# Attention heads: even and odd key tiles on the two row halves, and scores moved up to 896 columns at a time

## The chip, the cores and the metric

The kernel runs on one core of a Trainium2 chip. The metric is the device time of one execution in microseconds; the figure given for a kernel is the median of its runs. A core has five engines that each work through their own instructions in order: TensorE (PE, with its weight loads as PEld), VectorE (DVE), ScalarE (ACT), GpSimd (POOL) and SyncE (SP, which issues most DMAs). PE writes to PSUM, eight banks of 512 f32 columns on each of 128 rows; everything else here lies in SBUF or DRAM.

## The reference

The input is 3327 rows of 256 numbers and an adjacency matrix. Two layers run one after the other. Layer 0 is a graph convolution and a mixture of experts with the best two of eight; layer 1 is a graph attention and then the part that matters here, `_L1_ffn_ref`: causal attention with four heads of width 64, where each head has one key and one value projection but four query projections ("experts"):

```python
q = jnp.einsum('bnsd,neod->bneso', sx, wq)      # 4 heads, 4 experts each
k = jnp.einsum('bnsd,nod->bnso', sx, wk)
v = jnp.einsum('bnsd,nod->bnso', sx, wv)
scores = jnp.einsum('bnesd,bntd->bnest', q, k) * d ** 0.5 + causal
att = jax.nn.softmax(scores, axis=-1)
qkv = jnp.einsum('bnest,bntd->bnesd', att, v)
```

The four experts' results are mixed by a gate, added to the head's own input, normalised, sent through two small linear layers and normalised and gated again. All of it is in f32.

## The kernel before

The rows are padded to 26 tiles of 128 (`NT`, `P`). The graph layers and the expert layer come first and are the same in both kernels, except that the value rows are stored for the heads in another order (`keep_values`, line 914). The heads stage is `heads` (line 999 on).

A *unit* is one query tile `t` and one head `h`: 104 units, in order of `t`. A unit has the keys of tiles 0 to `t`. `span` cuts them into `t // 4 + 1` *chunks* of at most four tiles (512 columns). For each chunk:

- `fill` (PE): scores `pqk`, one matmul for each of four experts, 128 queries by up to 512 keys, contraction 64. Keys stand twice, on rows 0 to 63 and again on rows 64 to 127 (`kt`, `wk` has its columns twice). Queries of experts 0 and 2 stand on the upper half of the rows, of 1 and 3 on the lower. So two experts' matmuls run side by side on the two halves of PE. Each expert's scores take one PSUM bank of the four in the pool `ps`.
- `drain` (DVE): takes each expert's scores out of PSUM to the score buffer `sc` and keeps the row maximum (`mx`); in a unit's last chunk it adds the causal mask as well. After the last chunk a reduction gives `anmax`, the negative maximum over the unit.
- `weigh` (ACT): the exponentials, in place, one instruction per expert, with their sums in `den`.
- `values` (SP): four DMAs that bring the chunk's value rows `vr` from DRAM; three buffers.
- `turn` (DVE): transposes the whole chunk, four experts at once, in 32x32 blocks.
- `attend` (PE): products of weights and values in 32-row pieces, added up in `po` (four more banks).

After a unit's last chunk `over` takes `po` out and `back` turns it with `ptO`. Two generators run beside the units, a step at a time: `prepare` (with `heads_of`) makes the next tile's keys, values and queries (`psxt`, `pv`, `pk`, `pq`), and `tail` finishes a tile (gates, norms, `ph`, `pfg`). Their small matmuls use the same four banks; `empty` takes them out of PSUM, on ACT or DVE by a running estimate of both loads.

The order of the instructions on every engine is the order in which this program writes them (`InOrder`, line 50, holds each engine to it). The main loop goes over the chunks: in round `k` it drains up to `wanted(k)`, attends chunk `k`, turns chunk `k + 1`, loads the values of chunk `k + 2`, weighs chunk `k + 2`, and ends with the fill of the next chunk. `extra(k)` moves weighing and turning one round further ahead for units of tile 5 up to about tile 23. Chunks of the next unit are drained early, since the exponentials need the maximum over the whole unit; that is what the nine score buffers of 512 columns are for.

Of the kernel before, what the change touches and what calls it, by code (L numbers as in the profile page):

```python
# [12 lines left out]
F32 = mybir.dt.float32  # L13
# [5 lines left out]
ALU = mybir.AluOpType  # L19
# [11 lines left out]
NEG = -1e30  # L31

# [17 lines left out]
class InOrder:  # L50
# [44 lines left out]
    def __init__(self, tc):  # L95
        nc = tc.nc
        self.tensor, self.vector = self.Engine(tc, nc.tensor), self.Engine(tc, nc.vector)
        self.scalar, self.gpsimd = self.Engine(tc, nc.scalar), self.Engine(tc, nc.gpsimd)
        self.sync = self.Engine(tc, nc.sync)


class Net:
# [811 lines left out]
    def keep_values(self, nc, vs, t, v):  # L914

        for b in range(4):
            nc.sync.dma_start(
                out=vs[:, :, 4 * t + b, :].rearrange("h r d -> r h d"),
                in_=v[ds(32 * b, 32), :].rearrange("p (h d) -> p h d", h=4),
            )  # L920

    def heads_fixed(self, one, nc):
# [50 lines left out]
        for k in range(2):  # L973
# [12 lines left out]
        mask = one.tile([P, BLK], F32, name="mask")  # L986
# [4 lines left out]
            out=mask[:, BLK - P :], in_=mask[:, BLK - P :], compare_op=ALU.is_ge, fill=NEG, base=0,  # L991
# [7 lines left out]
    def heads(self, xs, vs, out):  # L999
# [3 lines left out]
        with ExitStack() as ctx:  # L1003
            one = ctx.enter_context(tc.tile_pool(name="at", bufs=1))
            self.work = ctx.enter_context(tc.tile_pool(name="atw", bufs=2))
            scp = ctx.enter_context(tc.tile_pool(name="ats", bufs=9))
# [4 lines left out]
            ps = ctx.enter_context(tc.tile_pool(name="psm", bufs=4, space=PSUM))  # L1011
# [5 lines left out]
            kt = one.tile([P, 4, NP], F32, name="kt")  # L1017
# [82 lines left out]
            def heads_of(t, res, sxt, nz=None, v=None):  # L1100
# [11 lines left out]
                for c in range(2):  # L1112
                    for s in range(2):
# [3 lines left out]
                        )  # L1117
                for s in range(2):
                    empty(kt[:, s::2, ts(t, P)], pp[s], D)
# [3 lines left out]
                if t < AHEAD:  # L1123

                    qt = scp.tile([P, 4, BLK], F32, tag="sc", name="qts")[:, :, : 2 * P]
                    qt = qt.rearrange("p h (i q) -> p h i q", i=2)
                else:
                    qt = tl.tile([P, 4, 2, P], F32, tag="qt", name="qt")
# [9 lines left out]
                for s in range(2):  # L1138
                    empty(qt[:, s::2, :, :], pp[s], BLK, 8.0)
                yield  # L1140
                sx = tl.tile([P, D], F32, tag="sx", name="sx", bufs=4)
# [29 lines left out]
            def span(t, g):  # L1171


                n = t // 4 + 1
                lo, hi = (t + 1) * g // n, (t + 1) * (g + 1) // n
                return lo, hi - lo

            def fill(u, g):

                t, h = u["t"], u["h"]  # L1180
                lo, n = span(t, g)
                n *= P
                pq = u["pq"] = []
                for i in range(2):
                    pq += [ps.tile([P, BLK], F32, tag="b", name="pqk") for _ in range(2)]
                    for k in range(2):
                        r = ds(64 * k, 64)
                        nc.tensor.matmul(
                            pq[2 * i + k][:, :n], u["qt"][r, h, i, :], kt[r, h, ds(lo * P, n)],
                            start=True, stop=True,  # L1190
                        )

            def drain(u, g):

                n = span(u["t"], g)[1] * P
                last = g == u["t"] // 4
                if g == 0:
                    u["sc"] = {}
                    u["mx"] = sm.tile([P, 4, 8], F32, tag="mx", name="mx", bufs=3)
                sc = u["sc"][g] = scp.tile([P, 4, BLK], F32, tag="sc", name="sc")  # L1200
                for e in range(4):
                    s, m = u["pq"][e][:, :n], u["mx"][:, e, g : g + 1]
                    if last:
                        nc.vector.tensor_tensor_reduce(
                            sc[:, e, :n], s, mask[:, BLK - n :], 1.0, NEG, ALU.add, ALU.max, m
                        )
                    else:
                        nc.vector.tensor_scalar(
                            sc[:, e, :n], s, 1.0, None, ALU.mult, ALU.max, accum_out=m
                        )  # L1210
                    load["dve"] += 0.12 + 0.00104 * n
                if last:
                    u["nmax"] = sm.tile([P, 4], F32, tag="nmax", name="anmax")
                    nc.vector.tensor_reduce(
                        u["nmax"], u["mx"][:, :, : g + 1], AX.X, ALU.max, negate=True
# [3 lines left out]
            def weigh(u, g, experts):  # L1219

                n = span(u["t"], g)[1] * P
                q = ready[u["t"]]
                if u["h"] == g == 0 and 0 in experts:
                    q["den"] = sm.tile([P, 16, 7], F32, tag="den", name="aden", bufs=3)
                for k in experts:
                    e = u["sc"][g][:, k, :n]
                    nc.scalar.activation(
                        e, e, AF.Exp, bias=u["nmax"][:, k : k + 1],
                        accum_out=q["den"][:, 4 * u["h"] + k, g : g + 1],
# [3 lines left out]
            def values(u, g):  # L1233

                lo, n = (4 * i for i in span(u["t"], g))
                v = u["v", g] = vrp.tile([P, 16, 64], F32, tag="vr", name="vr")
                for q in range(4):
                    nc.sync.dma_start(out=v[ds(Q * q, Q), :n, :], in_=vs[u["h"], :, lo : lo + n, :])

            def turn(u, g):  # L1240


                n = span(u["t"], g)[1] * P
                w = u["sc"][g][:, :, :n]
                nc.vector.transpose(w, w)
                load["dve"] += 0.1 + 0.00417 * n
# [7 lines left out]
            def attend(u, g):  # L1254


                t = u["t"]
                w, v = u["sc"][g], u["v", g]
                lo, n = (4 * i for i in span(t, g))
                for b2 in range(0, n, 2):  # L1260
                    for k in range(2):
                        for q in range(4):
                            r, b = ds(Q * q, Q), b2 + k

                            after = 4 * t + q - lo
                            if b > after and t:
                                continue
                            nc.tensor.matmul(
                                po[ds(64 * k, 64), q, :, :], v[r, b, :], w[r, :, ts(b, Q)],
                                start=(g == b2 == 0), stop=(b + 2 > after if t else b2 == 2),  # L1270
                            )
# [133 lines left out]
            def tail(t, sx, qkv, glp, den):  # L1405
# [3 lines left out]
                nc.vector.tensor_reduce(rd, den[:, :, : t // 4 + 1], AX.X, ALU.add)  # L1409
# [104 lines left out]
            def last_shares(u):  # L1514
# [3 lines left out]
                    rd, ready[u["t"]]["den"][:, ds(4 * u["h"], 4), : u["t"] // 4 + 1], AX.X, ALU.add  # L1518
# [39 lines left out]
            def last_half(c, r):  # L1558
# [12 lines left out]
                if c:  # L1571
                    pg = r["pg"] = ps.tile([P, 4], F32, tag="b", name="pfg")
# [37 lines left out]
            units = [dict(t=t, h=h) for t in range(NT) for h in range(4)]  # L1610
            chunks = [(u, g) for u in units for g in range(u["t"] // 4 + 1)]
# [19 lines left out]
            def fill_next():  # L1631
                nonlocal filled
                if filled < len(chunks):
                    u, g = chunks[filled]
                    if g == 0:
                        begin(u)
                    fill(u, g)
                    filled += 1

            def drain_to(n):  # L1640
                nonlocal drained
                while drained < min(n, len(chunks)):
                    if filled == drained:
                        fill_next()
                    drain(*chunks[drained])
                    drained += 1

            def extra(k):

                t = chunks[min(k + 3, len(chunks) - 1)][0]["t"]  # L1650
# [606 lines left out]
```

## Time and profile before

| what | value |
|---|---|
| median of 3 runs | 2826.27 us (2823.85 to 2828.45) |
| the profiled execution: time | 2829.15 us |
| the profiled execution: span | 2827.4 us |
| granted TensorE clock, mean | 0.982 |
| busy: PE / DVE / ACT / POOL | 2641.5 / 2374.8 / 1809.2 / 1119.6 us |
| drains without the mask | 1152, 653.2 us |
| drains with the mask | 416, 242.0 us |
| transposes of scores | 392, 816.2 us |
| exponentials | 1568, 1041.4 us |
| score matmuls `pqk` | 766.7 us |
| products `po` | 756.4 us |

Busy time is the sum of an engine's instruction records; matmuls are pipelined and their ends are modelled, so PE's is not exact. All recorded instructions carry line 61, the helper that issues them, so groups are told apart by their tiles. The first `anmax` starts 960.7 us after the span's start: from there on the heads run.

### The profile page before, as it was taken

What the parts mean: (1) busy time and instruction counts of PE and PEld (TensorE: products, weight loads), DVE (VectorE), ACT (ScalarE), POOL (GpSimd) and SP (SyncE); (2) the same over time, 40 slices, a digit from 0 to 9 for tenths busy, and PEclk for the clock granted to TensorE, in tenths of its full rate; (3) what the DMA queues carried; (4) which work ended last, traced back from release to release, by engine and by line L of the source; (5) the groups of instructions that cost most, each with busy time, mean ns of one, the idle gap of its engine ahead of it and who ended that gap; (6) DMA issues with size and microseconds to landing.
All of it is one profiled execution on the core that took longest, in us unless ns stands there. A gap on an engine that the chain in (4) does not pass through costs nothing.

```text
span 2827.4 us, 124885 instructions
## 1 busy us (share of the span) xinstructions
PE 2641.5 (93%) x53338; PEld 1959.8 (69%) x53338; DVE 2374.8 (84%) x5517; ACT 1809.2 (64%) x5161; POOL 1119.6 (40%) x1597
## 2 busy tenths in 40 slices
PE   7999988878989999999999999999999999999986
PEld 5888877767767776676666666666666666666654
DVE  5114643599999798999999999999999999999997
ACT  5541135555555577777777776777767777776774
POOL 5655744532243157654444333333223222222121
PEclk9999999989999999999999999999999999999997
DMA  7997568647775333433433443444434444434432
GB/s 268 378 383 241 192 224 261 208 177 265 272 264 185 94 91 94 118 106 113 117 110 113 121 123 109 121 117 122 117 115 119 121 119 117 124 118 119 117 105 80
DMA packets 257947, 449.28 MB, mean 159 GB/s; under 512 B 58768, under 2 KB 156432, under 8 KB 257264
## 3 DMA queue, kind: packets, MB, share of 16 engines
q1 hardware_dynamic: 245104, 417.11, 47.1%
q0 software_dynamic: 6480, 17.76, 1.6%
q8 instruction: 419, 6.86, 1.0%
q10 hardware_dynamic: 5808, 6.44, 0.7%
q14 instruction: 136, 1.11, 0.1%
HBM read 392.98 MB, written 25.88 MB: 148 GB/s over the span
## 4 chain that ended last, share of the span: by engine, by line
DVE 38%; PE 28%; ACT 3%; issue 1%; DMA 1%; POOL 1%; SPq 0%; POOLq 0%; DVEq 0%; ACTq 0%
DVE sc L61 34%; PE pqk L61 10%; PE po L61 9%; PE acc L61 3%; PE ptO L61 2%; ACT sc L61 2%; DMA pan<-in_adjt_dram 1%; PE psxt L61 1%; DVE p L61 1%; PE pq L61 1%; ACT sq L61 0%; PE pt L61 0%; PE ph L61 0%; DVE sg L61 0%; PE pk L61 0%
## 5 line engine op out<-in xcount | busy, mean ns | idle before, releaser
L61 ACT ACTIVATE sc<-sc,anmax 128x512 f32<-128x512 f32 (+3 forms) x1568 | 1041.4, 669 | 102.0 <-DVE anmax L61 102.0
L61 PEld LDWEIGHTS po<-sc,vr 32*64 32x64 f32 x43728 | 659.9, 131 | 298.7 <-issue 135.1
L61 DVE STREAM_TRANSPOSE sc<-sc 128x2048 f32<-128x2048 f32 (+3 forms) x392 | 816.2, 2082 | 9.2 <-ACT sc L61 9.1
L61 PE MATMUL po<-sc,vr 32*64 32x128 f32 x43728 | 756.4, 276 | 33.0 <-DVE sc L61 26.1
L61 PE MATMUL pqk<-kt,qt 64*128 64x512 f32 (+1 forms) x2944 | 766.7, 586 | 20.3 <-DVE fgs L61 7.2
L61 DVE TENSOR_SCALAR_CACHE_REDUCE sc<-pqk 128x512 f32<-128x512 f32 (+2 forms) x1152 | 653.2, 622 | 26.5 <-PE pqk L61 24.7
L61 PEld LDWEIGHTS pqk<-kt,qt 64*128 64x128 f32 x2944 | 315.0, 186 | 243.6 <-issue 84.2
L61 PE MATMUL acc<-wh,p 128*128 128x257 f32 x1352 | 308.5, 386 | 35.7 <-DVE p L61 35.5
L61 PEld LDWEIGHTS acc<-wh,p 128*128 128x128 f32 x1352 | 254.4, 191 | 89.8 <-DVE p L61 53.2
L61 ACT ACTIVATION_READ_ACCUMULATOR sc<-sc,anmax 128x1 f32 x1568 | 299.8, 191 | 0.0
L61 PE MATMUL acc<-y,pan 128*128 128x256 f32 x1352 | 296.0, 380 | 0.8 <-ACT rstd L61 0.5
L61 POOL TENSOR_TENSOR ot<-ot,sxd 128x512 f32<-128x512 f32 x83 | 106.1, 1278 | 440.0 <-ACT ot L61 434.9
L61 PEld LDWEIGHTS acc<-y,pan 128*128 128x128 f32 x1352 | 255.5, 190 | 35.2 <-ACT rstd L61 0.9
L61 DVE CUSTOM_DVE_ANT_0 sc<-pqk,mask 128x512 f32<-128x512 f32 (+3 forms) x416 | 242.0, 636 | 20.8 <-PE pqk L61 20.4
L61 ACT ACTIVATE u<-u,d 128x512 f32<-128x512 f32 (+1 forms) x182 | 125.1, 688 | 154.7 <-DVE u L61 154.7
L61 DVE SCALAR_TENSOR_TENSOR p<-pan,u 128x512 f32<-128x512 f32 (+1 forms) x182 | 127.6, 701 | 10.5 <-PE acc L61 6.0
L61 DVE SCALAR_TENSOR_TENSOR u<-bc,d 128x512 f32<-128x512 f32 (+1 forms) x182 | 136.2, 749 | 0.1
L61 ACT ACTIVATE ar<-ar 128x1664 f32<-128x1664 f32 x52 | 82.5, 1588 | 80.6 <-DMA ar<-in_adj_dram 80.6
L61 DVE TENSOR_SCALAR y<-y,dinv 128x256 f32<-128x256 f32 x26 | 14.0, 537 | 134.0 <-POOL dinv L61 133.8
L61 PE MATMUL ptO<-igw,ot 128*128 128x68 f32 x832 | 116.9, 284 | 4.4 <-DVE sc L61 2.1
L61 PEld LDWEIGHTS ptO<-igw,ot 128*128 128x128 f32 x832 | 102.6, 194 | 23.3 <-issue 15.4
L61 ACT COPY qkv<-ptO 128x272 f32<-128x272 f32 x103 | 39.3, 382 | 121.1 <-PE ptO L61 121.0
(381 smaller groups left out, 3196.9 us busy)
## 6 DMA issues: line engine op xcount, KB each, us to landing
vr<-vs SPq DMA_DIRECT2D x976, 128.0 KB
ar<-in_adj_dram SPq DMA_DIRECT2D x104, 832.0 KB
vr<-vs SPq DMA_DIRECT2D x544, 96.0 KB
pan<-in_adjt_dram SPq DMA_DIRECT2D x156, 256.0 KB
pan<-in_adjt_dram SPq DMA_DIRECT2D x26, 1024.0 KB
pan<-in_adjt_dram SPq DMA_DIRECT2D x20, 832.0 KB
w1e<-w SPq DMA_DIRECT2D x59, 256.0 KB
took<-places SPq DMA_DIRECT2D x59, 129.0 KB
```

The lines of the kernel that those rows point to most:

```text
L61: made = make(*args, **kw)
```

## The change

Keys and queries change their places on the rows, and the unit of work for DVE and ACT becomes wider.

- `kt` has half the columns: keys of even tiles stand on rows 0 to 63, of odd tiles on rows 64 to 127. The matmuls `pk` are as before; each copy into `kt` writes one half of the rows.
- Queries are needed on both halves. `qt` gets a further dimension, and two DMAs on SP in `heads_of` copy each half to the other. For tile 2 a part of `kt` that is still free serves as `qt`.
- `doubles(t)` cuts a unit's keys into `ceil((t + 1) / 7)` *doubles* of at most seven tiles (896 columns, `WIDE`). In a double the tiles of one parity are one half and those of the other parity the other. One expert's scores of a double are two matmuls, one per half, that run on the two halves of PE into two neighbouring banks, so that the columns lie side by side.
- The pool of four banks becomes two pairs (`Pairs`); small matmuls get half a pair each.
- Drains and exponentials take a whole double of one expert, up to 896 columns, in one instruction. The mask is 896 columns wide. Six score buffers of 896 columns take the place of nine of 512.
- Transposes, values and products go in *rounds*: one round for a double of at most four tiles, else one round for each half. Value rows are stored with even tiles first (`place`), and each half of a round is loaded with four DMAs.
- Scores are filled and drained in *pieces* of two experts, each with a round by which it is due; the main loop is written anew around that, and starts four rounds before the first product.

The core of the diff:

```diff
+WIDE = 7 * P
+def place(t):
+    return t % 2 * (NT // 2) + t // 2
+def doubles(t):
+    n = -(-(t + 1) // 7)
+    out = []
+    for d in range(n):
+        tiles = range((t + 1) * d // n, (t + 1) * (d + 1) // n)
+        halves = [[i for i in tiles if i % 2 == p] for p in ((t + 1) % 2, t % 2)]
+        out.append([h for h in halves if h])
+    return out
+class Pairs:
+    def pair(self, name):
+        self.rest = None
+        return self.pool.tile([P, 2, BLK], F32, tag="b", name=name)
+    def tile(self, shape, dtype, tag, name):
+        if self.rest is None:
+            both = self.pair(name)
+            v, self.rest = both[:, 0, :], both[:, 1, :]
+        else:
+            v, self.rest = self.rest, None
...
-            scp = ctx.enter_context(tc.tile_pool(name="ats", bufs=9))
+            scp = ctx.enter_context(tc.tile_pool(name="ats", bufs=6))
-            ps = ctx.enter_context(tc.tile_pool(name="psm", bufs=4, space=PSUM))
+            ps = Pairs(ctx.enter_context(tc.tile_pool(name="psm", bufs=2, space=PSUM)))
-            kt = one.tile([P, 4, NP], F32, name="kt")
+            kt = one.tile([P, 4, NP // 2], F32, name="kt")
...
+                r = ds(64 * (t % 2), 64)
                 for s in range(2):
-                    empty(kt[:, s::2, ts(t, P)], pp[s], D)
+                    empty(kt[r, s::2, ts(t // 2, P)], pp[s][r, :, :], D)
...
+                for k in range(2):
+                    nc.sync.dma_start(
+                        out=qt[ds(64 - 64 * k, 64), :, 1, :, :], in_=qt[ds(64 * k, 64), :, 0, :, :]
+                    )
...
-            def fill(u, g):
+            def fill(g):
+                u, d, experts = g["u"], g["d"], g["experts"]
+                halves = u["doubles"][d]
+                g["pq"] = []
+                for e in experts:
+                    pair = ps.pair("pqk")
+                    lo = BLK
+                    for i, tiles in enumerate(halves):
+                        k, n = tiles[0] % 2, P * len(tiles)
                         r = ds(64 * k, 64)
+                        if i < len(halves) - 1:
+                            to, lo = pair[:, 0, BLK - n :], BLK - n
+                        else:
+                            to = pair[:, 1, :n]
                         nc.tensor.matmul(
+                            to, u["qt"][r, u["h"], int(e % 2 != k), e // 2, :],
+                            kt[r, u["h"], ds(tiles[0] // 2 * P, n)], start=True, stop=True,
                         )
...
+            def turn(r):
+                w = r["u"]["sc"][r["d"]][:, :, ds(r["lo"], r["n"])]
                 nc.vector.transpose(w, w)
...
+                    for k in range(2):
+                        at = len(rounds) - 1 if single else len(rounds) - 2 + k
+                        pieces.append(dict(
+                            u=u, d=d, experts=(2 * k, 2 * k + 1), double=count, round=at,
+                            due=at - (2 if single else 3), first=first, lead=lead,
+                        ))
...
+            for g in pieces:
+                g["by"] = g["round"] - len(g["u"]["rounds"]) + 1 - g["lead"]
...
             def extra(k):
-                t = chunks[min(k + 3, len(chunks) - 1)][0]["t"]
-                return int(chunks[k][0]["t"] >= 5 and t // 4 + 1 <= 6 or chunks[k][0] is units[-1])
+                k = min(max(k, 0), len(rounds) - 1)
+                far = rounds[min(k + 8, len(rounds) - 1)]["u"]["t"]
+                return int(rounds[k]["u"]["t"] >= 5 and far <= 20 or rounds[k]["u"] is units[-1])
...
+            for k in range(-4, len(rounds)):
+                want = wanted(k)
+                drain_to(min(want, drained + 1))
+                if k >= 0:
+                    attend(r)
+                if drained < want and filled == drained:
+                    fill_next()
...
+                    turn(rounds[flipped])
                     flipped += 1
+                drain_to(want)
...
+                if filled == drained < wanted(k + 1):
                     fill_next()
```

## The prediction

> **What bounds the kernel now.** I read the page's busy shares and chain first, then busy time by stretch, then the timeline of the heads stage, then the chain inside one stretch. The first score maximum stands at 960.7 us, so the heads are the last 1865 us, and the change touches only them.
>
> ```profile
> PE 2641.5 (93%) x53338; PEld 1959.8 (69%) x53338; DVE 2374.8 (84%) x5517; ACT 1809.2 (64%) x5161; POOL 1119.6 (40%) x1597
> ...
> DVE 38%; PE 28%; ACT 3%; issue 1%; DMA 1%; POOL 1%; SPq 0%; POOLq 0%; DVEq 0%; ACTq 0%
> ```
>
> The 84% of DVE is a mean over stages. By stretch (us, then PE, PEld, DVE, ACT, POOL):
>
> ```profile
> 1400.00:1600.00 200.00, 194.03 (x5294) 135.15 (x5298) 191.93 (x463) 147.84 (x461) 89.15 (x120) 1.00 0.40 114
> 2000.00:2200.00 200.00, 194.39 (x5609) 131.01 (x5612) 194.46 (x416) 150.17 (x484) 61.86 (x85) 0.99 0.41 118
> 2200.00:2400.00 200.00, 197.70 (x5658) 133.51 (x5645) 199.00 (x426) 153.91 (x486) 57.70 (x79) 1.00 0.41 118
> ```
>
> Two engines are full at once; ACT has a quarter free. The prices come from the timeline (start, duration):
>
> ```profile
> 2600.56 0.69 DVE L61 TENSOR_SCALAR_CACHE_REDUCE sc<-pqk 128x512 f32<-128x512 f32 x1
> 2601.17 0.69 DVE L61 TENSOR_SCALAR_CACHE_REDUCE sc<-pqk 128x512 f32<-128x512 f32 x1
> 2601.79 0.69 DVE L61 TENSOR_SCALAR_CACHE_REDUCE sc<-pqk 128x512 f32<-128x512 f32 x1
> 2602.40 2.31 DVE L61 STREAM_TRANSPOSE sc<-sc 128x2048 f32<-128x2048 f32 x1
> 2605.55 0.56 DVE L61 TENSOR_SCALAR_CACHE_REDUCE sc<-pqk 128x384 f32<-128x384 f32 x1
> 2606.03 0.56 DVE L61 TENSOR_SCALAR_CACHE_REDUCE sc<-pqk 128x384 f32<-128x384 f32 x1
> 2606.51 1.77 DVE L61 STREAM_TRANSPOSE sc<-sc 128x1536 f32<-128x1536 f32 x1
> ```
>
> Drains start 0.61 us apart at 512 columns and 0.48 at 384: 0.133 us per key tile and some 0.08 fixed. PE's prices stand in the chain of 2000 to 2040 us:
>
> ```profile
> 2000.27 1.92 PE pqk L61 x8
> 2002.18 1.58 PE po L61 x93
> 2003.77 1.04 PE ptO L61 x8
> 2004.80 1.92 PE pqk L61 x8
> 2006.72 2.02 PE po L61 x125
> ```
>
> Eight score records (four experts in two passes each, two row halves side by side) over four tiles take 1.92 us, 0.24 per tile and pair of experts; the products of four tiles take 2.02, 0.51 per tile.
>
> **Drains.** The built program of the changed kernel holds 992 drains instead of 1568, over the same columns. 576 fewer at 0.075 us is -43 us of DVE. [...]
>
> **Transposes.** A double of 5 to 7 tiles is turned in two parts: 468 transposes for 392, each with about 0.07 us between its columns (2048 elements at 1.04 ns in a 2.23 us spacing leave 0.1; the 1536 form leaves less). +5 us. DVE's net is -38 us of some 1800.
>
> **Score matmuls.** Before, two experts ran on the two row halves over the same tiles, so both halves were always full. Now one expert's even and odd tiles share the halves, and the longer part sets the time. The built program has 208 experts' doubles of 4+3 tiles (4 steps instead of 3.5), 224 of 3+2 (3 instead of 2.5), 32 uneven ones at tiles 0 and 2; 448 of 3+3 lose nothing. That is 232 steps more on 2808; at 0.24 us, +56 us of PE. It lies beside DVE only as far as PE has room.
>
> **Which engine is then the floor.** Per head of query tile t I add the prices. PE: 0.49 per tile of scores, 0.51 of products, 1.04 for ptO, and 1.8 for a quarter of the tile's small matmuls (psxt 1.09, pv 0.64, pk 0.71, pq 1.16, two ph 0.71, four pt 0.39, pfg 0.51). DVE: drains, transposes, and 0.8 (1.3 below tile 16) for maxima and tails. The measured time of a head is the distance between maxima:
>
> ```profile
> 2408.12 0.18 DVE L61 TENSOR_REDUCE anmax<-mx 128x4 f32<-128x24 f32 x1
> 2435.68 0.18 DVE L61 TENSOR_REDUCE anmax<-mx 128x4 f32<-128x24 f32 x1
> 2466.21 0.18 DVE L61 TENSOR_REDUCE anmax<-mx 128x4 f32<-128x24 f32 x1
> ```
>
> Floors DVE/PE before, then after, then measured before (mean of a tile's four heads): t=9: 13.3/12.8, 13.1/13.8, 13.6. t=14: 19.0/17.8, 19.0/19.3, 18.6. t=19: 24.3/22.8, 23.8/23.8, 24.0. t=20: 25.8/23.8, 24.9/25.3, 26.4. t=23: 29.0/26.8, 28.6/26.8, 28.6. The larger floor, over all 104 heads, falls by only 15 us: at half the tiles PE becomes the larger. **-15 us.**
>
> **Waits when two floors meet.** Before, where the floors lie within 0.6 us (t=4 to 11) heads ran 0.55 us over the larger one on average; where DVE leads by over 1 us (t=12 to 24), 0.0. After, 10 of the 14 tiles from 12 on have floors within 0.9 us. 40 heads x 0.55 = **+22 us**; bounds 0 and +45 (double). The cause is visible in the rounds. With one drain piece of two experts and one transpose per round, DVE needs 2 x 2.03 + 2.23 + 1.7 = 8.0 us for a 7-tile double, PE 2 x 1.92 + 3.5 = 7.4 and 0.7 of small matmuls: no slack. For the same 7 tiles it was 8.3 against 7.0 + 0.7. PSUM remains four banks, now two pairs, and a small matmul takes half a pair that ACT must empty before the second expert's scores can be written; before, it took one bank in four, which the last expert waited for at about the same moment, so I charge nothing more for that.
>
> **Query copies.** Each query tile now also goes to the other row half by two DMAs on SP. For tiles 0, 1, 5, 6 and 8 the PE order has the first scores directly behind that tile's pq matmuls, and for tile 3 nearly so: PE waits for the landing.
>
> ```profile
> L61 SPq DMA_DIRECT2D sxd<-nz x104: 596/605/1773, 901.1 to 2557.3; - x104
> ```
>
> This copy from SBUF to SBUF is the nearest row: 0.6 us an issue, and in the packet records of 958 to 962 us the last landing follows the last issue by 1.15. Two issues and a landing are 2.4 us; six tiles, +14, less what DVE still has queued: **+10 us** (bounds 0, +14). From tile 9 on other work stands between; the cover is a round of 4 us or more. While SP holds a copy for ACT's qt, the next vr pieces stand behind it; they are read two rounds later, and without that cover each tile would pay another 1.2 us (two issues). [...]
>
> **Values.** SP issues vr pieces 0.46 us apart. A round with two halves in one buffer needs 8 issues: 3.7 us, and the tile's other 13 issues at 0.6 add 2 per head, 5.7 in all against heads of 5.2 to 6.6 at tiles 1 to 3. **+2 us** (0, +6). Elsewhere four issues fit a round.
>
> **Look-ahead.** The extra round of weighing and turning ahead now ends at about tile 20 instead of 23. Before, tile 24, the first without it, ran 0.75 us per head worse against its floor than tiles 21 to 23. Twelve heads, 9 us, partly counted in the waits: **+5** (0, +9).
>
> **Exponentials.** 992 instead of 1568 at some 0.3 us fixed (0.60 spacing at 384, 0.70 at 512) is -170 us on ACT, which is not the bound. What can return is PE's waiting for ACT to empty a bank:
>
> ```profile
> PEld pqk L61 <- ACT qt L61: 10.6, 28, 2.2
> PEld pqk L61 <- ACT qkv L61: 6.6, 11, 1.4
> PEld pqk L61 <- ACT sxt L61: 5.4, 16, 0.9
> ```
>
> With sx 4.5 that is 27 us in all, and each exponential gets longer (about 1.0 us), so **-4** (0, -13). The key copies (the same columns on half the rows), the wider mask and the reordered value rows cost nothing on the path: ACT, POOL and DMA (0.41 busy) cover them. Uncovered, the mask's 384 more columns would be 1.6 us once, by POOL's 1.09 us for a 128x256 row.
>
> Sum: -15 + 22 + 10 + 2 + 5 - 4 = **+20 us**. The profiled execution took 2829.15 us (span 2827.4 and 1.75 outside), 2.9 above the median 2826.27. 2849 on its scale is 2846 on the median's.
>
> **Rivals.**
> (a) Faster: DVE stays the bound and the fixed drain time comes off whole, 2826 - 38 = 2788. For it: DVE busy 199 of 200 in 2200 to 2400, and 3+3 doubles, nearly half of all, which cost PE nothing. Against it: PE is at 194 to 198 in the same stretches. It decides if small matmuls fit into PE's idle time without delaying the next scores, waits under 0.1 us per head. With half of the saving, 2807.
> (b) Gain and loss cancel: -15 and waits of +15, copies hidden: 2826.
> (c) Much slower: two PSUM pairs make DVE and PE take turns. If each of the 468 rounds shows 0.2 us more, 94 stands in place of the 22: 2918; from 0.05 us a round on it exceeds the forecast. For it: a pair comes free only after a whole drain of 1.0 us. Against: one transpose of 1.7 to 2.2 us per round lies between drains and covers the fill.
> (d) The change does not do what it says: excluded, the built program has 896-column drains and exponentials.
>
> **Chances.** Forecast 0.45, (a) with its half form 0.35, (b) 0.12, (c) 0.08. The measurement tells 0.2%, 5.7 us. The forecast's own range, from its bounds without all favourable ends at once, is 2828 to 2880. The range runs from (a) at 2787 to 2888; left out are a gain above DVE's own saving and most of (c). Faster 0.35, same 0.11 (most of (b)), slower 0.54.
>
> **What would show it.** Right: DVE's busy total down by about 38 and its share of the heads below 96%; PE idle under 2% from tile 12 on, PE's share of the chain up; heads at tiles 14, 9 and 15 longer than before, at 16 and 24 shorter; pqk waiting for a qt copy at the tiles named. Wrong: DVE still at 98% with shorter heads everywhere (a), or DVE waiting for pqk in every round (c).

## The result and the profile after

The changed kernel takes 3033.18 us, the median of six executions (3026.43 to 3039.57), against 2826.23 us before. The ratio is 1.073 (95% interval 1.071 to 1.075): 7.3% or 207 us slower. The forecast was 2846 us in a range of 2787 to 2888. The direction was right and the size was off by a factor of ten. Below, "so many us above before" is always a kernel's ratio less one, times 2826, so that runs from different chips can stand side by side. The profiled execution has a span of 3030.9 us and a mean granted clock of 0.957, against 0.982.

The page's busy totals of the changed kernel, and its chain by engine:

```profile
PE 2736.3 (90%) x54138; PEld 2036.5 (67%) x54138; DVE 2357.0 (78%) x4441; ACT 1659.2 (55%) x4009; POOL 1117.1 (37%) x1597
...
PE 35%; DVE 22%; ACT 5%; issue 2%; POOL 1%; DMA 1%; POOLq 0%; ACTq 0%; SPq 0%; DVEq 0%
```

DVE's total fell, by 18 us, and PE took the chain over from it (35% against 28%), as forecast. But the busy shares fell too: the new time is waiting, and work of PE at a lower clock. Busy time by stretch of the changed kernel shows where (us, then PE, PEld, DVE, ACT, POOL, PE's clock, DMA share, GB/s):

```profile
960.00:1100.00 140.00, 112.74 (x1372) 86.16 (x1372) 72.30 (x209) 49.88 (x170) 23.12 (x30) 0.66 0.26 67
1100.00:1400.00 300.00, 244.70 (x5010) 175.98 (x5016) 192.84 (x395) 154.42 (x438) 151.73 (x209) 0.87 0.30 83
1400.00:1600.00 200.00, 189.17 (x5006) 131.27 (x4990) 179.58 (x331) 130.88 (x347) 99.31 (x137) 1.00 0.42 116
2000.00:2200.00 200.00, 191.97 (x5541) 129.89 (x5522) 188.15 (x286) 132.23 (x348) 66.57 (x93) 1.00 0.43 120
2200.00:2400.00 200.00, 192.96 (x5531) 132.76 (x5522) 186.29 (x261) 127.84 (x320) 55.69 (x75) 1.00 0.43 123
```

From 2000 us on both engines stand at 93 to 96.5%, where they had 97 to 99.5% before. Early, DVE is busy for 52 to 64% of the time and the clock is at 0.66 and 0.87. The same 36 heads, from the first score maximum of tile 0 to that of tile 9, before:

```profile
960.73:1266.33 305.60, 290.12 (x6411) 211.84 (x6409) 268.51 (x747) 224.78 (x755) 180.26 (x249) 0.98 0.35 98
```

and after:

```profile
962.62:1405.33 442.71, 359.74 (x6509) 263.48 (x6508) 269.23 (x607) 208.23 (x618) 176.39 (x243) 0.81 0.29 78
```

So 137 of the 207 us are lost there, and 65 on tiles 9 to 25 (1561 us before, 1626 after). In the early part PE's busy time grew by 69.6 us and its idle time from 15.5 to 83.0. By an estimate from these two lines the growth of busy time is nearly all clock: 359.74 us at 0.81 hold 68 us of lost clock, 290.12 at 0.98 hold 6. What DVE waits for, in its costliest groups over the whole kernel (busy, mean ns | idle before, releaser):

```profile
L80 DVE STREAM_TRANSPOSE sc<-sc 128x1536 f32<-128x1536 f32 (+3 forms) x468 | 829.4, 1773 | 18.9 <-ACT sc L80 18.9
L80 DVE TENSOR_SCALAR_CACHE_REDUCE sc<-pqk 128x768 f32<-128x768 f32 (+3 forms) x576 | 506.1, 911 | 87.0 <-PE pqk L80 85.6
L80 DVE CUSTOM_DVE_ANT_0 sc<-pqk,mask 128x768 f32<-128x768 f32 (+6 forms) x416 | 356.6, 887 | 150.8 <-PE pqk L80 148.9
```

The drains before:

```profile
L61 DVE TENSOR_SCALAR_CACHE_REDUCE sc<-pqk 128x512 f32<-128x512 f32 (+2 forms) x1152 | 653.2, 622 | 26.5 <-PE pqk L61 24.7
L61 DVE CUSTOM_DVE_ANT_0 sc<-pqk,mask 128x512 f32<-128x512 f32 (+3 forms) x416 | 242.0, 636 | 20.8 <-PE pqk L61 20.4
```

The drains take 862.7 us, against 895.2, and wait 234.5 us for PE's scores, against 45.1. The list of DVE's waits in the heads (total, times, longest) has them, first before, then after, as

```profile
DVE sc L61 <- PE pqk L61: 45.0, 52, 5.0
DVE sc L80 <- PE pqk L80: 234.6, 225, 11.0
```

And PE waits for DVE: here is the timeline of one head of tile 8 (start, duration, in brackets the idle time before and its releaser):

```profile
1333.45 0.69 DVE L80 TENSOR_SCALAR_CACHE_REDUCE sc<-pqk 128x512 f32<-128x512 f32 x1
...
1333.92 1.14 PE L80 MATMUL pqk<-kt,qt 64*128 64x256 f32 x8
...
1334.70 2.31 DVE L80 STREAM_TRANSPOSE sc<-sc 128x2048 f32<-128x2048 f32 x1 [0.55 <-ACT sc L80]
1336.93 0.65 DVE L80 TENSOR_SCALAR_CACHE_REDUCE sc<-pqk 128x512 f32<-128x512 f32 x1
...
1337.75 1.10 PE L80 MATMUL ptO<-igw,ot 128*128 128x68 f32 x8 [2.70 <-DVE sc L80]
...
1339.41 0.66 PE L80 MATMUL ptO<-ident,xn 128*128 128x128 f32 x2 [0.57 <-ACT qkv L80]
1340.00 2.93 PE L80 MATMUL pqk<-kt,qt 64*128 64x256 f32 x8
1341.69 0.82 DVE L80 CUSTOM_DVE_ANT_0 sc<-pqk,mask 128x640 f32<-128x640 f32 x1 [3.48 <-PE pqk L80]
```

One chain of waits can be followed here. PE writes the second piece's scores at 1333.92, and both pairs are full. DVE turns first (2.31 us) and drains after it, so ptO, which needs a pair, waits 2.70 us. Then the second half of ptO's pair, a transpose of `xn`, waits 0.57 us until ACT has emptied the first half. Then the next scores of the same shape take 2.93 us where they took 1.14: the granted clock is 0.50 from 1338.7 to 1345.5 us, and half the clock alone would make 2.3 us of it. Meanwhile DVE waits 3.48 us.

### The profile page after: what moved, and what is told of

Same layout as the page of the kernel before. It is cut to its first block, busy times and chain, and to the rows that moved or that the text cites. A ratio compares the mean times of both kernels' runs of the same rounds, so it can differ in the third digit from the quotient of the medians.

```text
span 3030.9 us, 125050 instructions
## 1 busy us (share of the span) xinstructions
PE 2736.3 (90%) x54138; PEld 2036.5 (67%) x54138; DVE 2357.0 (78%) x4441; ACT 1659.2 (55%) x4009; POOL 1117.1 (37%) x1597
## 4 chain that ended last, share of the span: by engine, by line
PE 35%; DVE 22%; ACT 5%; issue 2%; POOL 1%; DMA 1%; POOLq 0%; ACTq 0%; SPq 0%; DVEq 0%
DVE sc L80 20%; PE pqk L80 14%; PE po L80 14%; PE ptO L80 3%; ACT sc L80 2%; PE pt L80 1%; PE pq L80 1%; PE psxt L80 1%; ACT qt L80 1%; PE pv L80 1%; ACT sq L80 1%; PE ph L80 1%; DMA qt<-qt 0%; ACT ot L80 0%; POOL qkv L80 0%
## 5 line engine op out<-in xcount | busy, mean ns | idle before, releaser
L80 ACT ACTIVATE sc<-sc,anmax 128x768 f32<-128x768 f32 (+6 forms) x992 | 880.9, 891 | 111.9 <-DVE anmax L80 111.7
L80 PEld LDWEIGHTS po<-sc,vr 32*64 32x64 f32 x43728 | 683.3, 133 | 316.9 <-issue 139.2
L80 PE MATMUL pqk<-kt,qt 64*128 64x384 f32 (+3 forms) x3872 | 824.4, 515 | 62.3 <-DMA qt<-qt 19.8
L80 DVE STREAM_TRANSPOSE sc<-sc 128x1536 f32<-128x1536 f32 (+3 forms) x468 | 829.4, 1773 | 18.9 <-ACT sc L80 18.9
L80 PE MATMUL po<-sc,vr 32*64 32x128 f32 x43728 | 802.6, 281 | 35.7 <-DVE sc L80 19.8
L80 DVE TENSOR_SCALAR_CACHE_REDUCE sc<-pqk 128x768 f32<-128x768 f32 (+3 forms) x576 | 506.1, 911 | 87.0 <-PE pqk L80 85.6
L80 PEld LDWEIGHTS pqk<-kt,qt 64*128 64x128 f32 x3872 | 369.1, 193 | 279.1 <-issue 53.4
L80 DVE CUSTOM_DVE_ANT_0 sc<-pqk,mask 128x768 f32<-128x768 f32 (+6 forms) x416 | 356.6, 887 | 150.8 <-PE pqk L80 148.9
L80 ACT ACTIVATION_READ_ACCUMULATOR sc<-sc,anmax 128x1 f32 x992 | 188.8, 190 | 0.0
L80 PEld LDWEIGHTS ptO<-igw,ot 128*128 128x128 f32 x824 | 106.6, 202 | 47.5 <-issue 21.1
L80 ACT COPY ot<-po 128x512 f32<-128x512 f32 x83 | 48.4, 583 | 159.9 <-PE po L80 153.0
```

The costliest lines, as they stand in the source:

```text
L80: made = make(*args, **kw)
```

## The experiments

A *claim* below is a tile that has been taken from the pool of PSUM banks and not yet given back. The theory after this reading, called "turns": two pairs in place of four banks make PE and DVE take turns, most in the rounds of up to four tiles, and the clock follows the pauses. Its rivals: the query copies, the order of the work, the clock by itself.

| kernel | median us | ratio to before (95%) | us above before |
|---|---|---|---|
| changed | 3033.2 | 1.073 (1.071 to 1.075) | 207 |
| changed, no query copies | 3010.0 | 1.064 (1.063 to 1.066) | 181 |
| changed, drains ahead of transposes | 3003.9 | 1.063 (1.061 to 1.065) | 178 |
| changed, both drains at the round's start | 2993.3 | 1.060 (1.056 to 1.063) | 169 |
| changed, small products in whole pairs | 3009.0 | 1.064 (1.062 to 1.067) | 181 |
| changed, tile 14's `ot` on DVE | 3025.2 | 1.071 (1.069 to 1.074) | 202 |
| changed, drains split at the half | 3074.7 | 1.088 (1.086 to 1.090) | 248 |
| before, banks as two pairs | 2910.4 | 1.029 (1.027 to 1.031) | 82 |
| before, pairs, small products in whole ones | 2888.7 | 1.022 (1.019 to 1.026) | 63 |

**Pairs alone, in the kernel before.** This is rival (c) by itself: `Pairs` put into the kernel before, and nothing else. A pair holds the scores of two experts here, in the changed kernel those of one.

```diff
-            ps = ctx.enter_context(tc.tile_pool(name="psm", bufs=4, space=PSUM))
+            ps = Pairs(ctx.enter_context(tc.tile_pool(name="psm", bufs=2, space=PSUM)))
...
                 pq = u["pq"] = []
+                ps.rest = None
```

> The kernel before, with nothing changed but how the four banks are handed out: as two pairs, small products taking halves, the scores of two experts one pair; drains stay at up to 512 columns, keys and queries as before. My forecast charged the pairs nothing: 2826 to 2835 us. Theory 'turns', with two pairs in place of four banks as the cause by itself: 2870 to 2950, a good part of it in tiles 1 to 8. If it stays below 2840, the cause lies in the new order of drains and fills or in the shapes, not in the pairs.

It took 2910 us, 82 above before. DVE's groups in this kernel:

```profile
L61 DVE TENSOR_SCALAR_CACHE_REDUCE sc<-pqk 128x512 f32<-128x512 f32 (+2 forms) x1152 | 654.9, 622 | 63.8 <-PE pqk L61 62.1
L61 DVE CUSTOM_DVE_ANT_0 sc<-pqk,mask 128x512 f32<-128x512 f32 (+3 forms) x416 | 242.5, 637 | 50.8 <-PE pqk L61 50.0
```

The drains' busy time is what it was before (653.2 and 242.0 us), and their waits for scores went from 45 to 112 us. The price lies on all tiles: 42 us by the first maximum of tile 9, 41 after it.

**Whole pairs for small products**, in the same kernel. A second product in a pair was written only after ACT had emptied the first; this takes that wait away and leaves the two claims.

```diff
             v, self.rest = both[:, 0, :], both[:, 1, :]
+            if name != "pqk":
+                self.rest = None
```

> The kernel before with its banks handed out as two pairs, as in the run that took 2910 us, but with every small product taking a whole pair for itself, so that none waits until ScalarE has emptied the other half. Theory 'halves' (the price of the pairs is the second product of a pair waiting for the emptying of the first): 2850 to 2890. Theory 'two where there were four' (the price is that only two claims on PSUM can be open at a time): a second product in the same round now needs the other pair, and the scores behind it wait longer; 2920 to 2990.

2889 us (2887 to 2908), 63 above before (53 to 74): the shared halves were some 20 us of the 82. That lies just inside what "halves" expected, but the greater part is left: 63 us with two claims where there were four, each given back only when both its banks are empty. In the pairs kernel PE's waits from tile 0 to 8 began with this line, which is not among the greater ones in the run with whole pairs:

```profile
PE ptO L61 <- ACT qkv L61: 13.4, 25, 1.6
```

The same edit in the changed kernel:

> The changed kernel with every small product in a whole pair of its own, as in the run of the kernel before with pairs that went from 2910 to 2889 us by it. Theory 'halves' (the second product of a pair waits for the emptying of the first): 3000 to 3020 us. Theory 'two claims' (with whole pairs the small products hold up the scores): 3040 to 3080.

3009 us, 25 less than the changed kernel, as "halves" expected, and the waits of ptO for ACT's `qkv` are no longer listed among PE's waits in tiles 0 to 8.

**The query copies**, left out:

```diff
-                for k in range(2):
-                    nc.sync.dma_start(
-                        out=qt[ds(64 - 64 * k, 64), :, 1, :, :], in_=qt[ds(64 * k, 64), :, 0, :, :]
-                    )
...
-                            to, u["qt"][r, u["h"], int(e % 2 != k), e // 2, :],
+                            to, u["qt"][r, u["h"], 0, e // 2, :],
```

> The changed kernel without the copies of the queries to the other half of the rows: every score product reads the first placement, so the scores of half the products use another expert's queries; the number and the shapes of all other instructions stay. My forecast priced the wait for the copies at 10 us, so 3033 - 10 = 3023 us. Theory 'turns' (most of the 207 us come from TensorE and VectorE waiting for each other over two pairs of banks, in the rounds of up to four tiles above all): 3005 to 3020, since 13.6 us of TensorE's idle time in tiles 1 to 8 end with the copies' transfers and the clock falls after some of them. Theory 'copies' (the waits for them set the early tiles' pace and the low clock there): 2960 or less, and a granted clock of 0.95 or more between 963 and 1405 us, against 0.81.

3010 us: 25 us less, and the clock of tiles 0 to 8 stays low (0.82). In the changed kernel these were PE's greatest waits in that stretch (total, times, longest):

```profile
PE pqk L80 <- DMA qt<-qt: 13.6, 5, 5.9
PE ptO L80 <- ACT qkv L80: 11.8, 23, 0.8
PE ptO L80 <- DVE sc L80: 10.7, 6, 2.8
PE pq L80 <- ACT qt L80: 6.3, 5, 1.4
```

The copies are the first line, and only one of many. In tile 6 the copies and the scores behind them are

```profile
1193.55 1.26 SPq L80 DMA_DIRECT2D qt<-qt  x2
1197.03 1.22 PE L80 MATMUL pqk<-kt,qt 64*128 64x384 f32 x2 [5.95 <-DMA qt<-qt]
```

From the first issue to the scores that wait it is 3.5 us (3.3 to 4.5 in tiles 0, 1, 5 and 8), where my sum had 2.4 for two issues and a landing.

**The order of drains and transposes.** First the transposes were moved behind the second drain:

```diff
+                drain_to(want)
                 while flipped <= min(k + 1 + extra(k), len(rounds) - 1):
...
                     flipped += 1
-                drain_to(want)
```

> The changed kernel with both pieces of a round drained before the round's transposes, in place of one before and one behind them. Theory 'turns': in the rounds of up to four tiles (tiles 0 to 3, 7, half of 8) ptO waits some 2.5 us a head for the transpose that stands ahead of the second drain; 12 + 16 + 4 rounds x 1 to 2.3 us fall away, 2980 to 3010 us, with heads 1 to 3, 7 and 8 shorter and the others as they were. If the waits come from something else, the order of these two makes no difference: 3025 to 3040.

3004 us, 29 less. Tiles 3, 7 and 8 got 1.8 to 2.7 us a head shorter; tiles 1 and 2, named as well, did not (9.4 and 8.9 us before the edit, 9.3 and 9.1 with it). Then both pieces were drained at the start of the round, which puts the second piece's scores ahead of the attention products:

```diff
-                drain_to(min(want, drained + 1))
+                drain_to(want)
```

> The changed kernel with both pieces of a round drained at once at its start, so that the second piece's products go ahead of the round's attention products on TensorE, in place of behind them. Theory 'turns': in the rounds of up to four tiles VectorE then goes from the first piece to the second without waiting for the attention products, and the transpose runs beside them: more than the 29 us that came of moving the transpose alone, 2970 to 2995 us, tile 7 under 15 us a head against 18.1. If the start and tile 7 are slow for another reason (the copies, the clock alone): 2995 to 3035.

2993 us, 38 less than the changed kernel. Tile 7 fell from 18.1 to 14.8 us a head and ptO's waits for DVE left the list. The order was part of the change, and my sum has no term for it.

The two first edits together, drains ahead of transposes and no copies:

> The changed kernel without the copies of the queries and with both drains ahead of the transposes: the two edits that gave 23 and 29 us by themselves. If they act in different places: 3033 - 52 = 2981 us, and 70 us remain above the kernel before with pairs (2910). If both cut the same pauses, in which the clock falls: 2990 to 3000. The scores of half the products use another expert's queries.

2980 us (1.053, 1.051 to 1.054), 58 less than the changed kernel, where the two by themselves give 25 + 29: they do not cut the same waits.

**The clock.** Products of zeros were put where PE waits, first ahead of ptO in tiles 4 to 8:

```diff
                 if ended:
+                    for q in range(8 if u["t"] < 9 and not r["ends"] else 0):
+                        nc.tensor.matmul(
+                            po_all[:, q % 4, :P], self.ident, mask[:, :P], start=False, stop=False
+                        )
                     back(ended)
```

> The changed kernel with eight products of zeros (128x128, adding nothing) ahead of ptO in the heads of tiles 4 to 8, where TensorE waits; some 20 x 8 x 0.28 = 45 us more work for TensorE. Theory 'the clock falls because TensorE stands still': the granted clock of tiles 4 to 8 goes from 0.83 to 0.92 up to 0.97 or more, the other rows get shorter by 30 us, and the time is 3010 to 3035. Theory 'the clock follows something else': it stays under 0.93 there and the time is 3050 to 3080.

3047 us (1.077, 1.076 to 1.079), between the two expectations. In tile 7 the clock rose from 0.86 to 0.98 and its four heads got 3.6 us shorter, with 9 us more to do; tiles 5 and 8 reached only 0.93 and 0.89, and tiles 4 and 6 did not change. Then eight such products (`start=True, stop=True`) ahead of each round's attention products in tiles 0 to 3:

> The changed kernel with eight products of zeros (128x128, overwritten after) ahead of the attention products of each round of tiles 0 to 3: 16 x 8, 36 us of work at full clock. Theory 'the clock falls because TensorE stands still too often': the granted clock of tiles 0 to 2 rises from 0.50 to 0.67 up to 0.9 or more and the time is 3020 to 3045, the added work paid by the rows that get shorter. If the clock of the first tiles follows something else: it stays below 0.7, and the time is 3065 to 3100.

3042 us (1.075, 1.073 to 1.077), in the range expected if the clock follows PE's pauses, though the clock stayed under the 0.9 expected there. Tiles 0 to 2 in the changed kernel:

```profile
957.62:1047.60 89.98, 75.65 (x804) 58.98 (x805) 45.51 (x149) 30.53 (x112) 11.39 (x15) 0.57 0.25 66
```

and with the added products:

```profile
961.29:1055.54 94.25, 78.45 (x964) 64.24 (x965) 45.03 (x149) 30.55 (x112) 11.40 (x15) 0.85 0.24 63
```

The 160 PE records more are 80 products of two records each, some 27 us of busy time, and the stretch got only 4.3 us longer, since the clock went from 0.57 to 0.85. Shown is, for tiles 0 to 2 (0.57 to 0.85) and tile 7 (0.86 to 0.98), that work in the pauses keeps the clock up, so that the lost clock there is a consequence of the pauses and no cause beside them. For tiles 4 and 6, where the added work left the clock as it was, this is argued and not shown.

In the trace of the changed kernel the clock goes between 0.50 and 1.00, with 0.81 as the mean of 443 us; the wait in the timeline above, before it went from 1.00 to 0.50, was 2.70 us.

**One late operand.** At tile 14 PE waits once for POOL, which has a norm's operations ahead of `ot`. The timeline of the changed kernel:

```profile
1777.68 0.56 ACT L80 COPY ot<-po 128x512 f32<-128x512 f32 x1
...
1782.34 0.72 POOL L80 TENSOR_TENSOR fo<-fo,fnb 128x256 f32<-128x256 f32 x1
1783.02 1.26 POOL L80 TENSOR_TENSOR ot<-ot,sxd 128x512 f32<-128x512 f32 x1
...
1784.34 1.98 PE L80 MATMUL ptO<-igw,ot 128*128 128x68 f32 x8 [4.48 <-POOL ot L80]
```

ptO then takes 1.98 us, not 1.10: the clock again, 0.50 at that time. The edit is `u["t"] < 5 or u["t"] == 14` in `over`, which gives this multiplication to DVE.

> The changed kernel with the multiplication of po by sxd in tile 14 on VectorE, as in tiles 0 to 4, in place of ScalarE and GpSimd: ptO no longer waits for GpSimd behind the tail's norms. In tile 14 it waited 4.5 us once, and the rows behind it ran at half the clock for some 10 us more: theory 'one late operand and the clock behind it cost 8 to 10 us': 3021 to 3027. If the wait is taken over by another one: 3030 to 3040.

3025 us, 5 less by the ratio and 8 by the medians. The intervals of the two ratios overlap; the heads show it more surely: tile 14 went from 23.8 to 21.9 us a head, 7.5 us for four.

**What the wider drains are worth.** Each drain was split in two at the boundary of the halves, with everything else kept:

```diff
                 for e, s in zip(g["experts"], g["pq"]):
+                    at = 0
+                    for i, tiles in enumerate(halves):
+                        w = P * len(tiles)
...
+                                to, s[:, ds(at, w)], 1.0, None, ALU.mult, ALU.max, accum_out=m
```

> The changed kernel with each double's scores emptied by one instruction per half and expert (up to 512 columns) in place of one per expert (up to 896): 976 more instructions on VectorE, some 73 us by the 0.075 us that I took for one's fixed part. By the floors of my forecast (VectorE's is the larger one from tile 12 to 25, 14 tiles x 4 heads x about 20 more instructions x 0.075 us) it loses 40 to 75 us: 3073 to 3108. Theory 'turns' (what an emptying saves is given back in waits for pairs): 10 to 35 us, 3043 to 3068.

3075 us, 41 more. DVE's groups here:

```profile
L80 DVE TENSOR_SCALAR_CACHE_REDUCE sc<-pqk 128x384 f32<-128x384 f32 (+2 forms) x1152 | 550.4, 532 | 69.2 <-PE pqk L80 67.7
L80 DVE CUSTOM_DVE_ANT_0 sc<-pqk,mask 128x384 f32<-128x384 f32 (+3 forms) x816 | 387.2, 527 | 145.0 <-PE pqk L80 143.5
```

The drains take 937.6 us, 74.9 more for 976 more of them: 0.077 us each, and 41 of the 75 us reach the end. That is the low end of what the floors expected, and "turns", which had 10 to 35 us, missed: the saving is not given back in waits to the extent that it held. The wider drains do what they should; the change loses in spite of them.

**Other cuts of the tiles.** Sevens and a rest (`tiles = range(7 * d, min(7 * d + 7, t + 1))`):

> The changed kernel with the tiles of a query tile cut into sevens and a rest in place of equal parts: tile 7 goes 7 + 1 in place of 4 + 4, tile 8 7 + 2 in place of 4 + 5, tile 14 7 + 7 + 1, tile 21 7 + 7 + 7 + 1; the number of doubles is the same. Theory 'turns': the rounds of four tiles with two drains and a transpose of 2.3 us between them are the worst ones (tiles 7 and 8 take 7 us a head more than before, tile 9 1.7), so tile 7 falls from 18.1 to about 15.5 us a head and tile 8 from 20.1 to about 17: 3005 to 3020. If the loss comes with each double and not with the rounds of four: 3028 to 3050, as the rest of one tile costs a transpose and a score step more.

3146 us (1.112, 1.110 to 1.113), far outside both expectations. Tile 8 fell from 20.1 to 17.8 us a head, but tile 7, which should have fallen, rose from 18.1 to 19.7, and tiles 10, 11, 18 and 21 to 24 rose by 2.2 to 5.2. It has fewer rounds (432 for 468), so the number of rounds alone is not what is paid for. Rounds of unlike width in a row may be; that was not tried by itself.

**All mends together.** Both drains at the start, whole pairs, and tile 14's `ot` on DVE in one kernel; then the same without the copies:

> The changed kernel with three edits at once: both pieces drained at a round's start (40 us by itself), small products in whole pairs (24 us), tile 14's multiplication on VectorE (8 us). If they act apart from each other: 3033 - 72 = 2961 us. If they cut the same pauses, in which the clock falls: 2975 to 2995. If the loss above the kernel before came from these alone it would reach 2889 or less, which I do not expect: two claims on PSUM in place of four took the kernel before from 2826 to 2889 with none of the change's other parts.

2966 us (1.047, 1.045 to 1.049), 133 above before; single edits, 38 + 25 + 5 less than 207, would give 139.

> The same three edits, and the copies of the queries left out (23 us by itself; the scores of half the products use another expert's queries). Apart from each other: 2938 us. What then remains above the kernel before with whole pairs (2889 us) is the price of the uneven rounds and of the doubled score products, less the 42 us that the wider emptying saves: 2938 leaves 49 us for it. Below 2915 the four edits and the two claims are all there is; above 2955 the edits overlap.

2946 us (1.040, 1.037 to 1.043), 112 above before; the sum would be 114. The four edits add up. The copies are part of what the kernel needs, so this last one only measures. Nearly all that the four give lies in tiles 0 to 8, which went from 443 to 361 us (before: 306). Tiles 9 to 25 went from 1626 to 1619 us, against 1561: the late loss is hardly touched by them. In the kernel before, pairs alone added 41 us to those tiles, and with whole pairs 31.

**Sixes.** The kernel with three mends, with `if t in (8, 9, 14, 15, 21): tiles = range(6 * d, min(6 * d + 6, t + 1))`:

> The three edits that gave 2966 us, and tiles 8, 9, 14, 15 and 21 cut into sixes and a rest (6+3, 6+4, 6+6+3, 6+6+4, 6+6+6+4) in place of parts of four, five and six: where a double of five puts three tiles on one half of the rows and two on the other, TensorE works three steps for two and a half, and its two rounds are of three and two tiles. Tiles 9, 14, 15 and 21 lose 1.5 to 3.5 us a head against the kernel before. Theory 'doubles of five' (the step lost and the uneven rounds are what is left there): these four tiles get 1 to 2.5 us a head shorter, tile 8 stays or gains, 2925 to 2950 us. Theory 'any change of the width between rounds costs' (as the cut into sevens showed: 113 us more): no gain or a loss, 2960 to 3000.

2978 us (1.054, 1.051 to 1.057). In us per head:

| tile | before | changed | three mends | with sixes |
|---|---|---|---|---|
| 7 | 10.9 | 18.1 | 15.0 | 14.0 |
| 8 | 13.4 | 20.1 | 17.6 | 15.6 |
| 9 | 13.6 | 15.3 | 15.2 | 14.1 |
| 10 | 14.2 | 15.5 | 15.3 | 18.2 |
| 14 | 18.6 | 23.8 | 21.7 | 21.1 |
| 15 | 19.5 | 22.1 | 22.3 | 20.9 |
| 16 | 22.6 | 22.0 | 21.9 | 22.7 |
| 21 | 26.3 | 29.1 | 29.4 | 29.7 |
| 22 | 27.4 | 28.9 | 28.5 | 29.9 |

The column of three mends comes from its longest execution (2987.5 us), that of sixes from its shortest (2974.0), with a mean clock of 0.81 and 0.87 over tiles 0 to 8, so tiles 7 and 8 can't be compared closely. Tiles 9, 14 and 15 got shorter, by 12 us in all, and tiles 10, 16 and 22, where the number of rounds per head now steps up, got 20 us longer; tiles 9 to 25 together took 12 us more, as the medians do. The expectation of 2925 to 2950 fell; that of "any change of the width between rounds costs" holds. In the changed kernel, too, three of the worst tiles are those at which that number has just risen: 8 (from 2 to 3), 14 (from 4 to 6), 21 (from 6 to 8). At tile 7, the worst against before, it has not; there the number of doubles rises from 1 to 2. Drains are due a whole head ahead, so at such a step more scores must be written and drained in the rounds of the tile before; that this is the reason was argued from the code and not tried.

**The account.** 207 = 63 (two claims) + 25 (shared halves) + 38 (order) + 25 (copies) + 5 (late operand) - 41 (wider drains) + 92. The 63 were measured in the kernel before; that they are the same in the changed one is assumed. The last term is what no single edit holds, and its cause stays open: the longer score steps, rounds of unlike width, the tiles at which the number of rounds steps up, and the start are candidates. The runs show that the cut of the tiles moves it, and do not divide it further. None of the versions comes near the kernel before.

## Why the prediction was wrong

- **The step that failed** is the sentence on PSUM: a small matmul "takes half a pair that ACT must empty before the second expert's scores can be written; before, it took one bank in four [...] so I charge nothing more for that". Pairs alone cost 82 us in the kernel before, on every part of the heads. That is the largest price found, and less than half of the 187 us by which the forecast missed: the order of the loop (38 us) has no term in the sum either, and 92 us of the account are open. Rival (c) had the mechanism, with 0.2 us a round (94 us) and a chance of 0.08; over the 392 chunks of the kernel before, 82 us are 0.21 each. What I held against it, a transpose that "lies between drains and covers the fill", is the very instruction that stood in the way in the timeline above: with both pairs full, ptO waits behind it.
- **Waits when two floors meet, +22.** On tiles 9 to 25 my floors after sum to 22 us less than before, and the measured heads to 63 more. So, by these floors, the waits there are some 85 us, not 22. The 0.55 us a head came from heads with four banks; with two pairs the kernel before lost 41 us on the same tiles without any of the rest.
- **Tiles 0 to 8.** My sum has +7 us of floors, 10 for copies and 2 for values there. It was 137. I had not looked at what the new loop does in a round of at most four tiles, where two pieces of two experts replace one fill of four (38 us), nor asked what the clock does when PE pauses (some 60 us of the early loss goes through it, by the estimate of 68 us of lost clock against 6).
- **Query copies, +10 (0 to 14).** The waits are 19.8 us over six copies, in about the places named, and removing them is worth 25. The term was right in kind; what it had too small is the copy itself, 3.5 us from the first issue to the scores and not 2.4, and DVE's queue covered less than I took off. The remaining 5 us may be the low clock behind the waits (0.50 in the 3 us after those at 1197 and 1316 us); no run separates them.
- **Drains, -43.** The price of one drain more is right (0.077 us in the split kernel, 0.075 in the sum). A single row has a larger fixed part, some 0.15 us here (384 columns take 0.548 us, 512 take 0.681, so a key tile 0.133); neighbours overlap, as rows of 0.69 us start 0.61 us apart. The total fell by less than the price says: 862.7 against 895.2 us is -32. That fits drains that now follow each other by twos and not by fours, so that fewer overlap, but it was not tried. Transposes rose by 13 us, not 5. DVE's total fell by 18, not 38.
- **Values, +2, and exponentials, -4,** were not tried by themselves. PE's waits for ACT, which the term let shrink, grew instead: the shared halves are such waits.
- **What would show it.** DVE's share of the heads below 96% (85% from the first maximum on; it was 95% before), the chain going to PE, heads at 14, 9 and 15 longer and at 16 and 24 (30.8 to 30.2) shorter all came. PE idle under 2% from tile 12 on did not: from there to the last maximum it is 5.1%, and it was 3.2% before. "DVE waiting for pqk in every round", the sign named for (c), came in part: 225 waits in 468 rounds, against 52 before.

## What to carry to other kernels

Count claims on a buffer, not its bytes: here two claims in place of four, with nothing else changed, cost 82 us, and such a step can be tried by itself, in a few lines, in the kernel before. A saving on one engine should be weighed against the waits that two full engines then make for each other, with waits priced under the new buffering. Price a pause of PE with the clock of the rows behind it: of PE's 13 waits above 2 us (2.05 to 5.95) from the first score maximum of the changed kernel on, 12 were followed by a mean clock of 0.50 to 0.68 in the next 3 us, and one (2.25 us, at 1862 us) by 1.00.

## What the hardware showed that I had not expected

- PE's clock fell after short waits: after one of 2.70 us the next scores took 2.93 us, not 1.14, at a granted clock of 0.50 from 1338.7 to 1345.5 us. In the kernel before a wait of 1.65 us, at 1724 us, was followed by 3 us at 0.50. In tiles 0 to 2 PE was busy for 75.65 of 89.98 us and the mean clock was still 0.57.
- The time varies with the clock: the kernel with three mends took 2962 to 2988 us in five executions, longest where the mean clock was lowest (0.957) and within 2962 to 2966 at 0.970 to 0.973, while the kernel before stayed within 10 us on the same chip.
- Two products in the two banks of one pair, on different banks, still waited for each other's emptying, as if the pair were one tile for the wait: 0.57 us in the timeline above, 11.8 us in 23 waits in tiles 0 to 8. Whole pairs took these waits away and brought 20 to 25 us in all.
